# The gate's logits of a decoder layer: sixteen small products in the token loop, or one product for all tokens in the experts' part

## The chip, the cores and the metric

The kernel runs on one core of a Trainium2 chip. The metric is the device time of one execution in microseconds (us). All data and all products are in 32-bit floating point.

## The reference

A decoder layer over 16 sequences of 128 tokens with width 256: self-attention with 16 heads of 64, cross-attention with 16 heads of 16, then a mixture of 8 experts that adds up all experts and scales the sum by a gate. What concerns this change is the gate:

```python
xf = layernorm(x).reshape(-1, D)               # 2048 tokens, D = 256
logits = xf @ gate_w.T + gate_b                # E = 8 per token
ms = jnp.mean(logits * logits, axis=-1, keepdims=True)
logits = logits * jax.lax.rsqrt(ms + eps) * rms_w
gates = jax.nn.softmax(logits / 0.5, axis=-1)
g = gates.max(-1)                              # top 1
norm_g = g / (g + 1e-06)
h = gelu(einsum('nd,edh->neh', xf, w1) + b1)   # H = 512 per expert
y = einsum('neh,ehd->ned', h, w2) + b2
out = (y * norm_g[:, None, None]).sum(axis=1)
```

The logits thus need the normalized tokens and the gate's weights only, and the result `norm_g` is needed where the experts' sum is scaled and written.

## The kernel before, in words

The work is cut by sequence: `b` numbers the 16 blocks of 128 tokens. The kernel has three stretches.

**Slots.** `run_slots(B)` walks 16 slots; slot `s` holds self-attention of block `s`, cross-attention of blocks `s-1` and `s-2`, and the third layer norm of block `s-3`. Each step has a due time within a slot in the table `DUE`, and a heap puts all steps in the order of these times. That order is the program order on PE, DVE, ACT and POOL (`manual_schedule`). `expert_norm` (L670) transposes a normalized block to feature-major form in `xnT` [128, 2, 2048], which all of the experts' products read. `gate_logits(b)` (L678) follows at due time 26.93, after the second half of the keys of the next block (`k1`) and ahead of the cross-attention's keys (`ck`, L505). It makes two products: the 128x128 block of `xnT` stands in PE, and 8 columns of `wgt` move. Its PSUM tile comes from the ring `psum_mm` of four, which all projections and transposes of the slots share. At due time 27.6 DVE adds the bias into `lg[:, b, :]`.

**The written-out tail.** From L889 on the end of the token work (blocks 13 to 15) is laid out by hand between pieces of the experts' first layer (`pre_hidden`, L738) and second layer (`summed_plain`, L880). It holds the last three `gate_logits`. PE and ACT are in program order here, DVE is ordered by the planner.

**Experts.** `experts()` runs four groups `m` of 512 tokens over 16 blocks of hidden features `p`, with Strassen-like products of 256 columns at L993. One round is `hidden_first(p)` (banks `ha`, `hb`, `hf`, `he`; DVE then forms `u` at L1007 to L1009 out of them), part of the previous round's `summed`, `hidden_last(p)` (which adds into `ha`, `hf`, `he`; ACT applies the gelu, DVE forms `c` and the four `t`, L980 to L983), and the rest of `summed`. For `m = 0` the rounds begin at `p = PRE = 8`. Only PE is in program order; ACT, DVE and POOL are ordered by the planner. `gates()` (L692), some twenty small DVE instructions and one on ACT, turns `lg` into `gn` at `p = PRE + 2`; `gn` is first read at L1070 when the first group's sums are written, in group `m = 1`.

`ps_h` has one buffer for each of its banks. `hb` is written by one product a round and read by one DVE instruction (L1007). The weights `wgt` come on SP's DMA queue at L191, ahead of the later token blocks, the output weights `wo` and the experts' weights.

Of the kernel before, what the change touches and what calls it, by code (L numbers as in the profile page):

```python
# [11 lines left out]
F32 = mybir.dt.float32  # L12
# [3 lines left out]
ALU = mybir.AluOpType  # L16
AX = mybir.AxisListType

P = 128
B, T, D = 16, 128, 256  # L20
NT = B * T
KD = D // P
# [6 lines left out]
E, F = 8, 512  # L29
# [5 lines left out]
MT = 512  # L35
# [12 lines left out]
BO1, BO2, GTB, RMS = 0, 256, 512, 520  # L48
# [12 lines left out]
    LN3=18.94, SO=19.16, q1e=19.29, LN3c=19.36, cex0a=19.66, cmax1=19.89, cex0b=21.03,  # L61
    cr0a=21.36, cmul0a=22.23, cex1a=22.4, cr0b=22.6, CO=22.61, xsSO=22.81, bn=23.22,
    cmul0b=23.25, v1=23.47, xsCO=23.72, cex1b=23.78, cr1a=24.06, bn3=24.19, cmul1a=24.34,
    root=24.79, k1=25.19, ve1=25.39, gate=26.93, ke1=27.13, cr1b=27.14, ck=27.19, xn=27.27,
    cmul1b=27.42, lg=27.6, xn3=27.77, cke=28.26, ab2=28.44, early0=6.65, early1=6.7, early=7.9,
    cross=13.9, st0=14.3, st1=14.8, st2=15.6, st3=16.2, st4=17.4, st5=17.9, st6=18.4, st7=18.9,
    st8=20.0, st9=20.5, st10=21.0, st11=21.5, late=31.7,
)
# [5 lines left out]
def decoder_layer(  # L74
# [20 lines left out]
    nc = tc.nc  # L95
# [12 lines left out]
    const = ctx.enter_context(tc.tile_pool(name="const", bufs=1))  # L108
# [19 lines left out]
    def psum_mm(name):  # L128
        return ps_mm.tile([P, 512], F32, tag="mm", name=name)

    ident = const.tile([P, P], F32, tag="ident", name="ident")
# [9 lines left out]
    rowv = const.tile([P, NROW], F32, tag="rowv", name="rowv")  # L141
# [21 lines left out]
    for n, c0 in enumerate((BQ2, BK2)):  # L163
        for m in range(C2):
            for f in range(2):
                nc.gpsimd.dma_start(
                    out=bqk2[64 * f : 64 * f + 64, n, m : m + 1],
                    in_=cols[:, c0 + 2 * m + f : c0 + 2 * m + f + 1].rearrange(
                        "(a s) o -> a s o", s=32
                    )[:, :DH2],  # L170
# [12 lines left out]
    for n, w in ((1, wk2), (0, wq2)):  # L183
        for k in range(KD):
            nc.sync.dma_start(
                out=wx[:, n, k].rearrange("p (h d) -> p h d", d=DH2),
                in_=w[:, k].rearrange("p (h s) -> p h s", s=32)[:, :, :DH2],
            )
    nc.sync.dma_start(out=wx_vo[:, 1], in_=wo2)
    wgt = const.tile([P, KD, E], F32, tag="wgt", name="wgt")  # L190
    nc.sync.dma_start(out=wgt, in_=wg)  # L191

    for b0 in range(4, B, 4):
        load_tokens(b0, 4)
# [22 lines left out]
    xnT = const.tile([P, KD, NT], F32, tag="xnT", name="xnT")  # L217
# [15 lines left out]
    def at(name, f, *a):  # L233


        if now[0] is None:
            f(*a)
        else:
            heapq.heappush(events, (now[0] * SLOT + DUE[name], next(count), now[0], f, a))
# [435 lines left out]
            copy,  # L675
        )

    def gate_logits(b):  # L678
        mm = psum_mm("mm_g")
        for k in range(KD):  # L680
            nc.tensor.matmul(
                mm[:, :E],
                xnT[:, k, b * T : (b + 1) * T],
                wgt[:, k, :],
                start=(k == 0),
                stop=(k == KD - 1),
            )
        at(
            "lg", nc.vector.tensor_tensor, lg[:, b, :], mm[:, :E], rowv[:, GTB : GTB + E], ALU.add
        )  # L690

    def gates():  # L692
# [34 lines left out]
    PRE = 8  # L727
# [20 lines left out]
    def slot(s):  # L748


        for half in range(2):
            at(f"S{half}", self_scores, s, half)
            at(f"SV{'ab'[half]}", self_values, s, half)
            for n in range(2):
                at(f"T1{'ab'[half]}{n + 1}", self_transposed, s, half, n)
                if s >= 2:
                    at(f"T2{'ab'[half]}{n + 1}", cross_transposed, s - 2, half, n)
        at("SO", self_output, s)
        at("cvr", cross_value_rows, s)
        at("ck", cross_keys, s)  # L760
        normalize_outputs(s, s - 2 if s >= 2 else None)
        if s >= 1:
            at("LNx", cross_norm, s - 1)
            at("CQ", cross_queries, s - 1)
            at("CS", cross_scores, s - 1)
            at("CS", cross_softmax, s - 1)
        if s >= 2:
            at("CV", cross_values, s - 2)
            at("CO", cross_output, s - 2)
        if s >= 3:  # L770
            at("LN3", expert_norm, s - 3)
            at("gate", gate_logits, s - 3)
        if s + 2 < B:
            at("xn1", self_norm, s + 2)
            at("ab1", add_bias, s + 2, BO1)
            at("LN1", self_norm_transposed, s + 2)
        if s + 1 < B:
            for n in range(2):
                at(f"q{n}", queries, s + 1, n)
                at(f"k{n}", keys, s + 1, n)  # L780
                at(f"v{n}", values, s + 1, n)
        else:
            for n, name in enumerate(PRE_STEPS):
                copy = nc.vector.tensor_copy if name[0] == "q" else nc.scalar.copy
                out = f"q{name[1]}e" if name[0] == "q" else f"{name[0]}e{name[1]}"
                at(name, pre_hidden, n, copy, out)
        if s == 0:
            mv2 = variances(2)
            for i in range(2):
                at(f"early{i}", statistics, mv2[:, i, :], 2 + i)  # L790
            at("early", lambda: first.update(inverse_deviations(mv2, [2, 3])))
            at("cross", for_cross)
            mv = variances(B - 4)
            for i, name in enumerate(LATE_STATS):
                at(name, statistics, mv[:, i, :], 4 + i)

            def rest():
                first.update(inverse_deviations(mv, list(range(4, B))))

            at("late", rest)  # L800
# [88 lines left out]
    with tc.manual_schedule(  # L889
        engines={mybir.EngineType.PE, mybir.EngineType.Activation}  # L890
    ):
        b = B - 1
        a, v = nc.scalar.copy, nc.vector.tensor_copy
        for h in range(2):
            for n in range(2):
                cross_transposed(b - 1, h, n)
        pre_hidden(6, a)
        cross_values(b - 1)
        pre_hidden(7, a)
        cross_norm(b)  # L900
        cross_output(b - 1)
        expert_norm(b - 2)
        cross_queries(b)
        pre_hidden(8, a)
        cross_scores(b)
        normalize_outputs(None, b - 1)
        gate_logits(b - 2)
        pre_hidden(9, a)
        pre_hidden(10, a)
        cross_softmax(b)  # L910
        pre_hidden(11, v)
        expert_norm(b - 1, v)
        pre_hidden(12, v)
        gate_logits(b - 1)
        pre_hidden(13, v)
        for n in range(2):
            cross_transposed(b, 0, n)
        pre_hidden(14, v)
        pre_hidden(15, v)
        for n in range(2):  # L920
            cross_transposed(b, 1, n)
        scores.close()
        ps_y = ctx.enter_context(
            tc.tile_pool(name="ps_y", bufs=1, space=bass.MemoryType.PSUM, reuse_waits="tile")
        )
        ys = sums()

        def late(p):
            hidden_late(p)
            for k in range(KD):  # L930
                summed_plain(k, p, ys)

        late(0)
        cross_values(b)
        late(1)
        cross_output(b)
        normalize_outputs(None, b)
        late(2)
        late(3)
        expert_norm(b, v)  # L940
        late(4)
        gate_logits(b)
        for p in range(5, PRE):
            hidden_late(p)
    both.close()
# [147 lines left out]
    def experts():  # L1093

        nonlocal ys
        rest = None
        xr = token_factors(0)
        combine(2)  # L1100
        combine(3)
        for p in range(5, PRE - 1):
            for k in range(KD):
                summed_plain(k, p, ys)
        before = None
        for m in range(NT // MT):
            for p in range(0 if m else PRE, NP):
                if m and p == 0:
                    xr = token_factors(m)
                first = hidden_first(p, xr)  # L1110
                if before is None:
                    summed_plain(0, PRE - 1, ys)
                else:
                    if before[0] == 0:
                        ys = sums()
                    summed((1, 2, 3), *before, ys)
                now = p, hidden_last(p, xr, first)
                if before is None:
                    summed_plain(1, PRE - 1, ys)
                else:  # L1120
                    summed((7, 5, 6, 4), *before, ys)
                    if before[0] == NP - 1:
                        rest = finished(m - 1, ys, m == 1)
                if m == 0 and p in (PRE, PRE + 1):
                    combine(p - PRE)
                if m == 0 and p == PRE + 2:
                    gates()
                if p in (1, 2) and rest is not None:
                    rest(p - 1, "he")
                before = now  # L1130
        summed((1, 5, 7, 6, 2, 3, 4), *before, ys)
        rest = finished(m, ys, False)
        for i, bank in enumerate(("hb", "hf")):
            rest(i, bank)
# [67 lines left out]
```

## Time and profile before

| | us |
|---|---|
| runs shown | 879.74, 882.36, 882.36 (median 882.36) |
| profiled execution, its own time | 879.95 |
| profiled execution, span from first to last instruction | 878.2 |
| PE busy / DVE busy / ACT busy / POOL busy | 859.7 / 626.4 / 426.1 / 166.6 |
| gate's products: weight loads, matmuls | 64 each (each product in two passes) |

The profiled execution's time is 1.75 us over its span. PE's granted clock is 0.999. A matmul's duration in the trace holds its latency, and matmuls overlap; what one costs PE in a stream is read from the distance between starts, or from the chain of work that ended last, which is laid out without overlap. In that chain a row has its start, its length, the engine, the tile, the line and the number of instructions. In the timeline a row's length is from the first start to the last end, and a wait stands in brackets. PEld is the weight load, which runs beside the matmul before it. In a row's shape, 128\*32 means that a stationary operand of 128 rows and 32 columns stood in PE.

### The profile page before, as it was taken

Reading aid. Unit: us, or ns where it says so; the run is one execution under the profiler, and the core shown is the slowest. Engines: PE = TensorE matmul, PEld = TensorE weight load, DVE = VectorE, ACT = ScalarE, POOL = GpSimd, SP = SyncE. Lnnn points to the kernel's source line nnn. Section 1 sums busy time; section 2 is a strip of 40 time slices with the busy share of each in tenths; the row PEclk is TensorE's granted clock in tenths of the full one; section 3 lists DMA queues with packets and bytes.
Section 4 is the critical chain, followed back from the end, with each engine's and each line's share of the span. In section 5 each row is a group of like instructions: output and inputs, shape, how many; then the busy total and the mean of one; then the engine's idle time right before and its main releaser. Section 6 shows DMA issues by size and latency. Waiting matters only on the chain.

```text
span 878.2 us, 16053 instructions
## 1 busy us (share of the span) xinstructions
PE 859.7 (98%) x5984; PEld 719.8 (82%) x5984; DVE 626.4 (71%) x1528; ACT 426.1 (49%) x1622; POOL 166.6 (19%) x178
## 2 busy tenths in 40 slices
PE   6999999999999999999999999999999999999997
PEld 5788888888888888888876558878888888878886
DVE  3887787878777787778777489675667656575655
ACT  2366755576556756576553703434333333433332
POOL 4224423343323423342321100000000000000000
PEclk9999999999999999999999999999999999999999
DMA  8800000000000000000051000000000000000000
GB/s 219 253 1 14 1 14 2 2 13 2 8 7 2 13 1 1 14 1 2 6 188 49 13 37 0 1 14 12 1 0 1 25 1 1 0 13 13 1 1 24
DMA packets 19278, 21.30 MB, mean 24 GB/s; under 512 B 9520, under 2 KB 15680, under 8 KB 18560
## 3 DMA queue, kind: packets, MB, share of 16 engines
q1 hardware_dynamic: 17600, 18.89, 6.8%
q10 hardware_dynamic: 1232, 1.09, 0.5%
q8 instruction: 47, 0.77, 0.4%
q0 software_dynamic: 368, 0.30, 0.3%
q14 instruction: 31, 0.25, 0.1%
HBM read 18.16 MB, written 2.10 MB: 23 GB/s over the span
## 4 chain that ended last, share of the span: by engine, by line
PE 92%; DVE 4%; issue 1%; DMA 1%; ACT 1%; POOL 0%; DVEq 0%; ACTq 0%; POOLq 0%
PE y L993 18%; PE mm_qk L389 13%; PE mm_v L428 6%; PE tr_p L366 6%; PE mm_o L488 6%; PE he L993 5%; PE hf L993 5%; PE ha L993 5%; PE sc L444 4%; PE po L468 3%; PE y L880 3%; PE mm_h L738 3%; PE hb L993 3%; PE sc L578 2%; PE po L617 2%; PE mm_k L505 2%
## 5 line engine op out<-in xcount | busy, mean ns | idle before, releaser
L351 POOL TENSOR_TENSOR cpr<-cpr,rinv 128x512 f32<-128x512 f32 x64 | 68.5, 1071 | 221.4 <-DVE rinv L347 221.1
L336 ACT ACTIVATE cpr<-sc,nmax 128x128 f32<-128x128 f32 x256 | 89.9, 412 | 11.6 <-DVE nmax L330 11.6
L336 ACT ACTIVATE pr<-sc,nmax 128x128 f32<-128x128 f32 x256 | 90.8, 420 | 1.8 <-DVE nmax L330 1.8
L330 DVE TENSOR_REDUCE nmax<-sc 128x8 f32<-128x1024 f32 x64 | 76.5, 1215 | 9.7 <-PE sc L444 9.7
L351 POOL TENSOR_TENSOR pr<-pr,rinv 128x512 f32<-128x512 f32 x64 | 66.0, 1043 | 79.1 <-DVE rinv L347 78.7
L1023 DVE TENSOR_TENSOR c<-u,hf 128x256 f32<-128x256 f32 x56 | 23.5, 420 | 72.3 <-PE hf L993 72.3
L1022 ACT ACTIVATE h<-u,colv 128x256 f32<-128x256 f32 x56 | 28.4, 507 | 89.8 <-DVE u L1009 88.1
L389 PEld LDWEIGHTS mm_qk<-xnT,wk 128*128 128x128 f32 x512 | 62.4, 196 | 9.5 <-issue 6.3
L257 ACT COPY xnT<-tr_x 128x256 f32<-128x256 f32 x42 | 15.6, 373 | 111.2 <-PE tr_x L315 111.2
L993 PE MATMUL hf<-xt,w 128*128 128x256 f32 x224 | 66.7, 379 | 0.0
L993 PE MATMUL ha<-xnT,w 128*128 128x256 f32 x224 | 66.6, 379 | 0.0
L993 PE MATMUL y<-t,w 128*128 128x256 f32 x224 | 66.6, 379 | 0.0
L336 ACT ACTIVATION_READ_ACCUMULATOR pr<-sc,nmax 128x1 f32 x256 | 66.3, 259 | 0.0
L389 PE MATMUL mm_qk<-xnT,wk 128*128 128x128 f32 x512 | 64.0, 279 | 1.9 <-DMA wk<-in_wk 1.9
L336 ACT ACTIVATION_READ_ACCUMULATOR cpr<-sc,nmax 128x1 f32 x256 | 64.5, 252 | 0.0
L389 PE MATMUL mm_qk<-xnT,wq 128*128 128x128 f32 x512 | 63.9, 278 | 0.0
L1006 ACT COPY u<-ha 128x256 f32<-128x256 f32 x56 | 20.9, 373 | 87.2 <-PE ha L993 87.2
L389 PEld LDWEIGHTS mm_qk<-xnT,wq 128*128 128x128 f32 x512 | 59.8, 192 | 3.0 <-issue 2.9
L993 PE MATMUL y<-h,w 128*128 128x256 f32 x224 | 58.6, 381 | 1.6 <-DVE yT L1045 1.2
L428 PE MATMUL mm_v<-wv,xnT 128*128 128x512 f32 x128 | 60.2, 592 | 0.0
L488 PE MATMUL mm_o<-wo,atT 128*128 128x256 f32 x256 | 57.9, 379 | 0.0
L257 DVE COPY prT<-tr_p 128x512 f32<-128x512 f32 x64 | 39.7, 682 | 19.3 <-PE tr_p L366 19.3
(164 smaller groups left out, 1880.1 us busy)
## 6 DMA issues: line engine op xcount, KB each, us to landing
w<-in_w SPq DMA_DIRECT2D x8, 1024.0 KB, 5.3
ctx<-in_ctxT SPq DMA_DIRECT2D x8, 256.0 KB, 2.6
out_x<-ot SPq DMA_DIRECT2D x8, 256.0 KB, 2.1
xs<-in_x SPq DMA_DIRECT2D x3, 512.0 KB, 5.8
wk<-in_wk ACTq DMA_DIRECT2D x4, 256.0 KB, 8.7
wq<-in_wq SPq DMA_DIRECT2D x4, 256.0 KB, 10.3
wv<-in_wv SPq DMA_DIRECT2D x2, 512.0 KB, 7.7
wo<-in_wo SPq DMA_DIRECT2D x1, 1024.0 KB, 8.7
```

The source lines that it names most:

```text
L257: f(*a)
L330: nc.vector.tensor_reduce(w["nmax"], sc, AX.X, ALU.max, negate=True)
L336: nc.scalar.activation(w["pr"][:, i, :], sc[:, i, :], AF.Exp, bias=w["nmax"][:, i : i + 1], scale=1.0, accum_out=sums[:, j : j + 1],)
L351: nc.gpsimd.tensor_tensor(four, four, w["rinv", n].unsqueeze(2).broadcast_to([P, 4, T]), ALU.mult)
L366: nc.tensor.transpose(tr[:, j, :], w["pr"][:, 4 * n + j, :], ident)
L389: nc.tensor.matmul(mm[:, i, :], w[:, k, c * P : (c + 1) * P], xnT1[:, k, 0, :], start=(k == 0), stop=(k == KD - 1),)
L428: nc.tensor.matmul(mm, entry["xnT1", b][:, k, 0, :], wv[:, k, f], start=(k == 0), stop=(k == KD - 1),)
L444: nc.tensor.matmul(sc[:, j, c * T : (c + 1) * T], qT[r, 4 * half + c, :], kT[r, 4 * half + c, :], start=True, stop=True,)
L468: nc.tensor.matmul(po[j * DH1 : (j + 1) * DH1, c, :], v[:, h * DH1 : (h + 1) * DH1], prT[:, 4 * j + c, :], start=True, stop=True,)
L488: nc.tensor.matmul(mm[:, :D], atT[:, c, :], wo[:, c, :], start=(c == 0), stop=(c == C1 - 1))
L993: nc.tensor.matmul(out, left[p // q][n - 1][:, p % q], rights[n - 1], **flags)
L1022: nc.scalar.activation(h[:, 1, 1], u[:, 3], AF.Gelu, bias=col(B1 + 2 * p + 1))
```

## The change

The sixteen `gate_logits(b)` are gone, with their sixteen bias additions on DVE and their entries in `DUE`. `wgt` is widened to 32 columns for each half of the features, zeroed by POOL, and its first 8 columns are loaded. In the experts' part, for `m = 0`, after `hidden_last(PRE + 2)`, one `gate_logits()` makes all logits: the 128x32 weights stand in each of four column quarters of PE, and quarter `r` gets the 512 tokens of group `r` as its moving operand, so that the four quarters fill the four partition quarters of one PSUM bank (`hb`). ACT copies the bank to SBUF. One round later, after `hidden_last(PRE + 3)`, four transposes bring the logits back to token-major form in `hb`, and one DVE instruction adds the bias into all of `lg`. `gates()` moves from `p = PRE + 2` to `p = PRE + 3`.

```diff
-    wgt = const.tile([P, KD, E], F32, tag="wgt", name="wgt")
-    nc.sync.dma_start(out=wgt, in_=wg)
+    wgt = const.tile([P, KD, 32], F32, tag="wgt", name="wgt")
+    nc.gpsimd.memset(wgt, 0.0)
+    nc.sync.dma_start(out=wgt[:, :, :E], in_=wg)
...
-    def gate_logits(b):
-        mm = psum_mm("mm_g")
+    def gate_logits():
+        mm = ps_h.tile([P, MT], F32, tag="hb", name="mm_g")
         for k in range(KD):
-            nc.tensor.matmul(
-                mm[:, :E],
-                xnT[:, k, b * T : (b + 1) * T],
-                wgt[:, k, :],
-                start=(k == 0),
-                stop=(k == KD - 1),
-            )
-        at(
-            "lg", nc.vector.tensor_tensor, lg[:, b, :], mm[:, :E], rowv[:, GTB : GTB + E], ALU.add
+            for r in range(4):
+                nc.tensor.matmul(
+                    mm[32 * r : 32 * r + 32, :],
+                    wgt[:, k, :],
+                    xnT[:, k, r * MT : (r + 1) * MT],
+                    start=(k == 0),
+                    stop=(k == KD - 1),
+                    tile_position=(0, 32 * r),
+                )
+        lgT = yp.tile([P, MT], F32, tag="yT", name="lgT")
+        nc.scalar.copy(lgT, mm)
+        return lgT
+
+    def gate_transposed(lgT):
+        tr = ps_h.tile([P, 4, P], F32, tag="hb", name="tr_g")
+        for i in range(4):
+            nc.tensor.transpose(tr[:, i, :], lgT[:, i * T : (i + 1) * T], ident)
+        nc.vector.tensor_tensor(
+            lg.rearrange("p (r i) e -> p i r e", i=4),
+            tr.rearrange("p i (r w) -> p i r w", w=32)[:, :, :, :E],
+            rowv[:, GTB : GTB + E].unsqueeze(1).unsqueeze(1).broadcast_to([P, 4, 4, E]),
+            ALU.add,
         )
...
         if s >= 3:
             at("LN3", expert_norm, s - 3)
-            at("gate", gate_logits, s - 3)
...
         normalize_outputs(None, b - 1)
-        gate_logits(b - 2)
         pre_hidden(9, a)
...
         pre_hidden(12, v)
-        gate_logits(b - 1)
         pre_hidden(13, v)
...
         late(4)
-        gate_logits(b)
...
                 now = p, hidden_last(p, xr, first)
+                if m == 0 and p == PRE + 2:
+                    lgT = gate_logits()
+                if m == 0 and p == PRE + 3:
+                    gate_transposed(lgT)
...
-                if m == 0 and p == PRE + 2:
+                if m == 0 and p == PRE + 3:
                     gates()
```

More of the change, by code (lines that the diff above doesn't have):

```diff
@@ L63 @@
     cmul0b=23.25, v1=23.47, xsCO=23.72, cex1b=23.78, cr1a=24.06, bn3=24.19, cmul1a=24.34,
-    root=24.79, k1=25.19, ve1=25.39, gate=26.93, ke1=27.13, cr1b=27.14, ck=27.19, xn=27.27,
-    cmul1b=27.42, lg=27.6, xn3=27.77, cke=28.26, ab2=28.44, early0=6.65, early1=6.7, early=7.9,
+    root=24.79, k1=25.19, ve1=25.39, ke1=27.13, cr1b=27.14, ck=27.19, xn=27.27,
+    cmul1b=27.42, xn3=27.77, cke=28.26, ab2=28.44, early0=6.65, early1=6.7, early=7.9,
     cross=13.9, st0=14.3, st1=14.8, st2=15.6, st3=16.2, st4=17.4, st5=17.9, st6=18.4, st7=18.9,
```

## The prediction

> **What bounds the kernel now.** I read the page first (the engines' shares, the chain that ended last), then the chain in single stretches, then the groups by shape, then the timelines of PE and DVE where the new work goes.
>
> ```profile
> span 878.2 us, 16053 instructions
> ...
> PE 859.7 (98%) x5984; PEld 719.8 (82%) x5984; DVE 626.4 (71%) x1528; ACT 426.1 (49%) x1622; POOL 166.6 (19%) x178
> ...
> PE 92%; DVE 4%; issue 1%; DMA 1%; ACT 1%; POOL 0%; DVEq 0%; ACTq 0%; POOLq 0%
> ```
>
> PE is the chain nearly everywhere. What PE no longer does is time saved, except where the 4% of DVE lie. A steady slot, in the chain:
>
> ```profile
> 267.16 0.35 PE mm_g L681 x4
> 267.50 0.99 PE mm_k L505 x8
> ...
> 277.03 0.89 PE mm_q L556 x8
> ...
> 279.65 1.75 PE tr_p L366 x16
> ```
>
> The gate has 0.35 us, and the eight products behind it have 0.99, where the same eight-product shape (mm_q) without a gate ahead has 0.89. In slot 2, which has no gate yet, mm_k itself has
>
> ```profile
> 96.84 0.89 PE mm_k L505 x8
> ```
>
> So one gate costs 0.35 + 0.10 = 0.45 us of PE. A check on whole slots: self-attention's scores start at 69.87, 97.67 and 126.13, so the slot without gate and without the third norm's transposes took 27.80 and the next one 28.46; the difference, 0.66, is the gate's 0.45 and two transposes of 0.11.
>
> Two places are DVE's. In the last slot the chain runs on DVE from 450.5 to 468.4:
>
> ```profile
> 450.52 1.34 DVE prT L257 x3
> ...
> 466.80 0.97 DVE xn L306
> 467.78 0.61 DVE cprT L245
> 468.52 0.63 PE tr_p L366 x4
> ```
>
> And in the experts' first rounds DVE works without a gap from 509.8 to 549.2 (weight combinations, then gates()), and once PE waits for it:
>
> ```profile
> 531.29 0.70 PE L993 MATMUL he<-xnT,w1c 128*128 128x256 f32 x2 [0.23 <-DVE u L1009]
> ```
>
> **What is removed.** Slots 3 to 14: 12 x 0.45 = 5.40. Nothing takes the gate's place there: DVE waits for the scores at the slot's head (0.44 us idle ahead of nmax at 269.6), and its own work ahead of that shrinks too, since the bias addition (158 ns, 0.08 from its start to the next one's) goes; the keys' copy on ACT (267.19 to 268.33) would still be done ahead of the second half of the scores (from 269.4, then 269.0). Taking a tile out of the PSUM ring of four only makes later tiles wait for earlier releases.
>
> Slot 15's gate lies at 465.5 within the DVE chain: only the 0.08 of DVE counts. The three gates of the tail: 0.34 each plus the slower start of what follows, as in
>
> ```profile
> 497.30 1.01 PE po L617 x32
> 498.31 3.63 PE y L880 x8
> ...
> 513.32 0.34 PE mm_g L681 x4
> 513.67 6.97 PE y L880 x16
> ```
>
> where 16 passes at 0.43 would be 6.88: 0.43 together. Likewise 0.43 at 478.8 and 0.44 at 486.5. (The first shows 0.54, but 0.20 of it is the way from the row-tiled scores, which the next product will pay.) Sum 1.30. Between the last scores and their transposes PE loses 0.87 of cover; POOL's half-0 product ends at 487.93 and its transposes start at 488.94, so 1.0 of margin remains 0.1 to 0.3. Removed in all: 5.40 + 0.08 + 1.30 = 6.8 us.
>
> Given back: the last gate lies after DVE's unbroken stretch has begun, which itself shrinks by 0.07 only. At 531.29 PE already waits, so 0.43 - 0.07 = 0.36 turns into a longer wait there.
>
> **Here a rule speaks against the change.** The row first: four gate passes of 8 columns take 0.45 us, 0.11 each, while their 128-column weight loads are
>
> ```profile
> L681 PEld LDWEIGHTS mm_g<-wgt,xnT 128*128 128x128 f32 x64 | 8.7, 192 | 1.8 <-issue 1.0 <-ACT pre L245 0.3 <-DVE root_t L278 0.2
> L681 PE MATMUL mm_g<-wgt,xnT 128*128 128x8 f32 x64 | 8.3, 237 | 0.0
> ```
>
> The Trainium skill's page "TensorEngine Tiling (Array Packing)", section Performance Considerations, Instruction Overhead, says that a matmul has about 60 cycles of overhead, so that one of 1 column takes as long as one of 60; at the 2.4 GHz that "TensorE: Matmul & The Clock Gate" states that is 25 ns. By it the 64 passes would be worth 1.6 us, and the change would lose about 1.6 us (1.6 removed, 3.2 added and given back). The row decides: the distance is 0.11, the weight load's, and I take 0.45.
>
> **What is added on PE.** Eight products in two passes, 16 passes of 512 columns at 0.43 (3.44 for eight y passes): 6.9 us one after the other. The nearest row for four column quarters is the cross-attention's values, 128\*32, also with the quarter as the inner loop: 32 passes in 1.01 us, starts 0.026 apart, where a 128-column pass alone needs 0.108. So four run at a time. Sixteen passes / 4 x 0.43 = 1.72, and the way into and out of the quarters: 1.01 - 32 x 0.108 / 4 = 0.15 before, 3.63 - 3.44 = 0.19 after. Together 2.06. The skill gives less on column tiles: "TensorE: Matmul & The Clock Gate", Part 3, Measured speedup, has 2.38 for three and 3.07 for four row tiles. With 3.07 it would be 2.25 + 0.34 = 2.6. I take the row, 2.06; 512 moving columns in four quarters are shown nowhere, so the ends are 1.9 and 7.2.
>
> Four transposes: 4 x 1.75 / 16 = 0.44.
>
> **Waits added.** (a) Round 11's product into hb waits until ACT has copied the logits (0.59 for 128x512). Between them PE has four y products and ha, 1.73 + 0.43 = 2.16; on ACT the copy stands behind round 10's gelus, which end 0.5 to 1 us ahead of it. Nothing; were ACT held 1.3 us longer, it would show. (b) Round 12's product into hb waits for the DVE addition out of hb (about 0.3, from the 128x128 gate rows at 284 to 292 ns). Behind hidden_last PE has 0.44 + 2.16. A later round shows where PE and DVE would be (timeline of each):
>
> ```profile
> 549.53 0.59 PE L993 MATMUL he<-xnT,w1c 128*128 128x256 f32 x2
> ...
> 552.12 0.59 PE L993 MATMUL hb<-xt,w1c 128*128 128x256 f32 x2
> ```
>
> ```profile
> 551.16 0.42 DVE L980 TENSOR_TENSOR t<-h 128x256 f32<-128x256 f32 x1 [0.57 <-ACT h L1026]
> ...
> 552.29 0.42 DVE L983 TENSOR_TENSOR t<-h,t 128x256 f32<-128x256 f32 x1
> ```
>
> Placed in the 0.57 of idle time ahead of the t's it costs nothing; behind the last t it ends near 553.0, where hb would be due at 552.56: 0.5 to 0.8 with the signal. I take 0.3. Queued behind it on DVE are the t's (next round's sums) and u. gates(), about 7 us of dependent small steps, moves from round 10 to 11 or 12, with DVE less loaded than now, and is needed some 25 us later: nothing. The new products read weights and tokens that have long been there.
>
> **At the start.** POOL's clearing of wgt comes at 10.8, ahead of the 128x1088 clears (1.02 each): about 0.1, covered, as POOL then waits 4.45 for DVE. SP's load at 23.66 now waits for that clear, 12 us after it: nothing. It has twice the pieces, 0.43 to perhaps 0.9 us of issue. Behind it stand token blocks, wo (issued 25.7, 8.7 to land, used at 37.65: 3.2 of margin), a context and the experts' weights. Nothing; if wo were late, the excess over 3.2.
>
> **Sum.** -6.8 + 0.36 + 2.06 + 0.44 + 0.3 = -3.6 us. The profiled execution took 879.95 (span 878.2 and 1.75 around it): 876.3. The median shown lies 2.4 above the profiled time, the mean of the three shown 1.5; I add 1.6 and say 878.
>
> **Rivals.**
> 1. *Half of the gain is eaten* (slots or DVE take it up: slot 15's chain spreads, the wide quarters reach 3 instead of 4, hb's wait is 0.8): -6.8 + 0.9 + 2.6 + 0.44 + 0.8 = -2.1, or 879.5; with less of the slots, 880.5. For: the margins at the tail's transposes and ahead of nmax are tenths. Against: the with-and-without slots.
> 2. *The quarters run one after the other*, slower than before: 6.9 + 0.34 in place of 2.06 at round 10. -3.6 + 5.2 = +1.6: 883. It decides when fewer than 1.5 passes run at a time. Against it stands L617; for it, that four wide moving streams of 128 partitions are untried.
> 3. *gates() goes as a block ahead of u (L1007)* in DVE's queue, as the planner orders it: 7.2 less the 1.3 of slack and 0.6 of idle, PE waits 5.3: +1.7, 883. It decides from 3.6 us of wait. Against: before, the planner threaded u between the gate's steps.
> 4. The change doing nothing it says can be excluded: the sixteen calls go.
>
> **Chances.** About 0.3% (2.6 us) is what a measurement here can tell from no change. The forecast 0.58, nearly all beyond 0.3%; rival 1 0.24, within it; rivals 2 and 3 0.07 and 0.06, and an unseen cost 0.05: half of these beyond 0.3% when measured, with the likeliest unseen cost in DVE's order. That gives faster 0.58, same 0.30, slower 0.12. The forecast's own range is 875 to 880; with rivals 1 and part of 2 and 3 the range is 874.5 to 882.5.
>
> **What would show it.** Right: no mm_g in the slots, mm_k at 0.89, score starts 28.0 apart; in round 10 a block of 16 passes 128\*32 with starts 0.11 apart and some 2.1 us in the chain; four tr_g at 0.11; a wait of at most 0.8 at hb in round 12; a longer wait at he in round 9. Wrong: starts 0.43 apart in the block, slots still 28.4 apart, or PE waiting microseconds for u or hb.

## The result, and the profile after

| | before | after |
|---|---|---|
| median of six runs, us | 882.0 | 877.83 |
| ratio, with its 95% interval | | 0.9959 (0.9946 to 0.9972) |
| profiled execution: time, span | 879.95, 878.2 | 877.13, 875.3 |

The change makes the kernel 0.41% faster (0.28 to 0.54), 3.6 us by the ratio; the medians alone are 4.2 apart. The two profiled executions differ by 2.8 (time) and 2.9 (span).

The lines of the page after the change that answer to the first fence of the prediction:

```profile
span 875.3 us, 15944 instructions
...
PE 856.2 (98%) x5940; PEld 713.6 (82%) x5940; DVE 627.5 (72%) x1513; ACT 425.5 (49%) x1623; POOL 166.8 (19%) x179
...
PE 89%; DVE 7%; issue 1%; ACT 1%; DMA 1%; POOL 0%; DVEq 0%; ACTq 0%; POOLq 0%
```

PE has lost 3.5 us of busy time and is as full as before; the chain leans on DVE for 7% in place of 4%, and most of the added share lies in the experts' first rounds. A steady slot in the chain of the kernel after (start, length, engine, tile, line):

```profile
265.10 0.89 PE mm_k L506 x8
265.99 1.99 PE sc L445 x32
...
294.00 1.99 PE sc L445 x32
```

The gate is gone, the keys behind it take 0.89, and the scores (`sc`) of two slots start 28.01 apart. The chain through DVE in the last slot has gained nothing:

```profile
461.21 1.40 DVE xn L307 x2
462.61 0.61 DVE cprT L246
463.35 0.63 PE tr_p L367 x4
```

The last two of these rows stand 5.17 us earlier than the same two in the prediction (467.78 and 468.52). That is what the twelve slots ahead had saved, 5.33, less the 0.16 by which this execution began later, and no more: DVE's 0.08 us did not show. The new block with the row ahead of it in round 9, again in the chain:

```profile
525.86 1.73 PE y L1004 x8
...
531.91 1.85 PE mm_g L684 x16
533.76 1.92 PE y L1004 x8
```

Sixteen passes take 1.85, and the eight passes of `y` behind them 1.92, where the same eight take 1.73 in round 9. In round 8, PE's timeline before and after:

```profile
524.35 0.59 PE L993 MATMUL hf<-xt,w 128*128 128x256 f32 x2
524.78 0.61 PE L993 MATMUL he<-xnT,w1c 128*128 128x256 f32 x2
```

```profile
517.84 0.59 PE L1004 MATMUL hf<-xt,w 128*128 128x256 f32 x2
518.55 0.70 PE L1004 MATMUL he<-xnT,w1c 128*128 128x256 f32 x2
```

The product into `he` came 0.43 after the one into `hf`, as in an unbroken stream; now it comes 0.71 after it. Later, with the waits in brackets:

```profile
525.16 0.70 PE L1004 MATMUL he<-xnT,w1c 128*128 128x256 f32 x2 [0.23 <-DVE u L1020]
...
539.84 0.60 PE L699 MATMUL tr_g<-ident,lgT 128*128 128x128 f32 x4
...
542.44 0.59 PE L1004 MATMUL hb<-xt,w1c 128*128 128x256 f32 x2
...
548.05 0.59 PE L1004 MATMUL ha<-xnT,w 128*128 128x256 f32 x2
...
552.10 0.70 PE L1004 MATMUL hf<-xt,w 128*128 128x256 f32 x2 [0.43 <-DVE u L1019]
...
554.88 0.59 PE L1004 MATMUL ha<-xnT,w 128*128 128x256 f32 x2
```

The wait in round 9, at 525.16, is the 0.23 that stood there before. The transposes cost their 0.44, the product into `hb` in round 12 follows without a wait, and in round 13 (548.05 to 554.88) PE waits for DVE where it did not before.

A table of where the time went, by starts in PE's timeline. A round runs from one product into `ha` that is followed by `hb` to the next such product. An undisturbed one takes 6.04; round 8, which has eight passes of 512 columns, takes 6.46 without any wait.

| stretch | before | after | difference | predicted |
|---|---|---|---|---|
| start of slot 3's scores | 97.67 | 97.83 | +0.16 | 0 |
| twelve slots to slot 15's scores | 341.30 | 335.97 | -5.33 | -5.40 |
| from there to round 8 | 81.50 | 80.17 | -1.33 | -1.38 |
| round 8 | 6.47 | 6.84 | +0.37 | +0.36 (in round 9) |
| rounds 10 and 11: block, transposes | 12.08 | 14.57 | +2.49 | +2.50 |
| round 12: wait at hb | 6.05 | 6.05 | 0.00 | +0.30 |
| round 13 | 6.04 | 6.83 | +0.79 | 0 |
| sum to round 14 | | | -2.85 | -3.62 |

### The profile page after: what moved, and what is told of

Read it like the earlier page. It is cut to its first block, busy times and chain, and to the rows that moved or that the text cites. A ratio compares the mean times of both kernels' runs of the same rounds, so it can differ in the third digit from the quotient of the medians.

```text
span 875.3 us, 15944 instructions
## 1 busy us (share of the span) xinstructions
PE 856.2 (98%) x5940; PEld 713.6 (82%) x5940; DVE 627.5 (72%) x1513; ACT 425.5 (49%) x1623; POOL 166.8 (19%) x179
## 4 chain that ended last, share of the span: by engine, by line
PE 89%; DVE 7%; issue 1%; ACT 1%; DMA 1%; POOL 0%; DVEq 0%; ACTq 0%; POOLq 0%
PE y L1004 18%; PE mm_qk L390 13%; PE mm_v L429 6%; PE tr_p L367 6%; PE mm_o L489 6%; PE he L1004 5%; PE hf L1004 5%; PE ha L1004 5%; PE sc L445 4%; PE po L469 3%; PE mm_h L753 3%; PE hb L1004 2%; PE sc L579 2%; PE po L618 2%; PE mm_q L557 2%; PE y L894 2%
```

## Experiments

The first 50 us differ by up to 4 us from one execution to the next whatever the kernel, which the section on the hardware explains. So the rounds and slots of the traces carry the verdicts here, and the ratios to the kernel before stand beside them where a kernel was run several times.

**The gates removed, nothing added.** Only the removal half of the change; `lg` is a constant, so the logits are left out.

```diff
+    nc.gpsimd.memset(lg, 0.5)
...
-            at("gate", gate_logits, s - 3)
...
-        gate_logits(b - 2)
...
-        gate_logits(b - 1)
...
-        gate_logits(b)
```

> The kernel before without its sixteen gate products and bias additions; the logits are a constant 0.5 set once, the rest including gates() in round 10 stays. Theory (PE is the bound, a gate is worth its four weight loads): 12 slots x 0.445, three in the tail x 0.44, nothing for the gate of slot 15, less 0.36 waited back at he in round 8 or 9: -6.3 us against before, slot 3 to 4 starts 28.0 apart instead of 28.46. Rival (a gate is worth its 8 moving columns[...]): -1.6 us. Rival (slots absorb it): slots stay over 28.2.

Ratio 0.9927 (0.9914 to 0.9940), or -6.4 us. In its chain:

```profile
268.05 1.99 PE sc L445 x32
...
296.06 1.99 PE sc L445 x32
```

In the trace the slots 3 to 13 are 28.01 or 28.02 long (28.46 before) and slot 14 is 27.79 (28.24), slot 15's scores to round 8 take 80.17 and round 8 takes 6.84: -5.3, -1.3 and +0.4, as in the table. A gate is worth 0.44, four times the 0.11 of a pass and not the 0.1 of the first rival; slots absorb nothing, except slot 15. One thing differs from what was expected: since the logits are a constant, the planner put gates() at 10.9 us and not in round 10. So the rounds 10 to 13 of this kernel, all at 6.04, say nothing about gates().

**The block and the transposes added, nothing removed.** The old gates stay in force, and the new logits go to a scratch tile; `gate_all` is the change's `gate_logits` with weights `wgp` of its own.

```diff
+    wgp = const.tile([P, KD, 32], F32, tag="wgp", name="wgp")
+    nc.gpsimd.memset(wgp, 0.0)
+    nc.sync.dma_start(out=wgp[:, :, :E], in_=wg)
...
+                if m == 0 and p == PRE + 2:
+                    lgT = gate_all()
+                if m == 0 and p == PRE + 3:
+                    gate_transposed(lgT)
```

> The kernel before with all its gates, plus the new block of 16 passes in round 10 and the four transposes and bias addition in round 11, which write a scratch tile that nothing reads; gates() stays in round 10. Theory (four quarters at a time): +2.05 for the block and +0.43 for the transposes, and no wait at round 13, since gates() is not moved: +2.5 us. Rival (gates() in its new place, not the block, is what costs DVE time at round 13): then this kernel shows no wait at hf in round 13. If the wait is there too, it comes from the addition's place on DVE.

In its chain:

```profile
540.07 1.85 PE mm_g L701 x16
541.92 1.92 PE y L1025 x8
...
548.16 0.44 PE tr_g L716 x4
```

Ratio 1.0024 (1.0016 to 1.0031), +2.1 us. Round 10 takes 8.09, round 11 6.48, round 13 6.04: +2.05, +0.44, and no wait. The two halves, -6.4 and +2.1, leave -4.3; the whole change measured -3.6. Within the intervals that is no contradiction. The 0.79 of round 13 appears in neither half: it comes only when gates() has to follow the new block.

**Does the order of the quarters matter?** The two loops of the block exchanged.

```diff
-        for k in range(KD):
-            for r in range(4):
+        for r in range(4):
+            for k in range(KD):
```

> The changed kernel with the block's loops exchanged: quarter outside, half of the features inside, so that the four passes of one quarter follow one another. Theory A (each quarter has its own queue, all sixteen passes are in sight at once): the block stays at about 1.85 us in the chain and 2.05 with the way out. Theory B (passes start strictly in order, and the next quarter starts only when the last pass of the one before has started): three passes of each quarter are waited for, 4 x 3 x 0.43 + 0.43 = 5.6 us, and the kernel is 3.7 us slower than the changed one.

In its chain:

```profile
531.33 1.87 PE mm_g L684 x16
```

1.87 against 1.85, and round 10 at 8.12 against 8.10. The number is theory A's: four passes of one quarter in a row hold up the other quarters no more than four quarters in turn. How PE queues the passes, the rows do not show.

**All products in one quarter.** The price of the rival in which the quarters do not run side by side. Three of four groups of logits are left out, and the two loops are exchanged as above.

```diff
-                    mm[32 * r : 32 * r + 32, :],
+                    mm[0:32, :],
...
-                    tile_position=(0, 32 * r),
+                    tile_position=(0, 0),
...
-        nc.scalar.copy(lgT, mm)
+        nc.gpsimd.memset(lgT, 0.0)
+        nc.scalar.copy(lgT[0:32], mm[0:32, :])
```

> The changed kernel with all eight products in the first column quarter, one group of tokens after the other over the same 32 partitions of the bank; only the last group's logits remain in it, the other rows are zero. Theory (passes of one quarter run one after the other): 16 x 0.43 = 6.9 us, 5.1 us more than the block in four quarters, the product into hb still covered, so span 875.3 + 5.1 = 880.4, slower than before by 2.2. Rival (the moving columns overlap also within a quarter): the block stays near 2 us.

In its chain:

```profile
531.42 6.99 PE mm_g L684 x16
538.41 1.92 PE y L1005 x8
```

6.99 for what four quarters do in 1.85, a factor of 3.8. Round 10 is 13.22, 5.13 longer than in the changed kernel, and the span is 880.0 (880.4 expected) against 878.2 in the trace of the kernel before.

**Sixteen times the moving columns.** The kernel before, with its gate weights padded to 128 moving columns.

```diff
-    wgt = const.tile([P, KD, E], F32, tag="wgt", name="wgt")
-    nc.sync.dma_start(out=wgt, in_=wg)
+    wgt = const.tile([P, KD, 128], F32, tag="wgt", name="wgt")
+    nc.gpsimd.memset(wgt, 0.0)
+    nc.sync.dma_start(out=wgt[:, :, :E], in_=wg)
...
-                mm[:, :E],
+                mm[:, :128],
```

> The kernel before with its gate weights widened to 128 moving columns by zeros, sixteen times as many moving columns in each of the 64 passes; the additions read the first 8 as before. Theory (a gate pass costs its 128-column weight load, 0.11, and up to 128 moving columns are covered by it): chain rows of the gate and the keys after it still sum to about 1.34, span within 0.7 us of 878.2. Rival (the moving columns count on top: 120 more at 0.84 ns each, 0.10 a pass): 64 x 0.10 = 6.4 us more, 884.6.

In its chain:

```profile
265.95 0.45 PE mm_g L682 x4
266.39 0.89 PE mm_k L506 x8
```

0.45 + 0.89 = 1.34, as 0.35 + 0.99 with 8 columns, and slots of 28.46 in both. The span, 877.0, is 0.5 under the expected range, since slot 0's scores start 1.2 earlier there. A pass with a 128-column stationary operand takes 0.11 whether 8 or 128 columns move. That is why the change pays: what stood in PE, 128 columns of tokens, now moves, in four quarters at once. That the 0.11 is the weight load, and not another floor under every pass, is the prediction's reading; no run here has a narrow stationary operand with few moving columns, which would part the two.

**Without gates().** The gate's steps from the logits to the scale are left out.

```diff
-                    gates()
+                    nc.vector.tensor_copy(gn, lg[:, :, 0])
```

> The changed kernel without the steps of gates(): the scale of the output is a plain copy of the first expert's logit, made after the addition. Theory (the wait at hf and he in round 13 comes from gates() on DVE): both waits are 0, span 0.75 us below the changed kernel's 875.3, 874.6; the waits at he in rounds 8 and 9 stay. Rival (round 13 waits for another reason, such as the block's shift of PE against DVE): the waits of 0.4 to 0.6 stay.

Round 13, between its first and the next round's first product in PE's timeline:

```profile
549.44 0.59 PE L1004 MATMUL ha<-xnT,w 128*128 128x256 f32 x2
...
555.49 0.59 PE L1004 MATMUL ha<-xnT,w 128*128 128x256 f32 x2
```

Round 13 takes 6.05, round 8 still 6.84, rounds 10 and 11 8.10 and 6.48. The wait comes from gates(). The span, 876.0, missed the expected 874.6, since slot 0 took 25.92 there and 24.30 in the changed kernel.

**The block ahead of round 8.** Where DVE is behind.

```diff
+        lgT = gate_logits()
         before = None
...
-                if m == 0 and p == PRE + 2:
-                    lgT = gate_logits()
```

> The changed kernel with the block of 16 passes moved from round 10 to just before round 8, where DVE is behind with the weight combinations; transposes and gates() stay in round 11. Theory (PE waits for DVE in rounds 8 and 9, 0.27 + 0.10 + 0.23 in all): the block gives DVE 2.05 us to catch up, so these waits go: about -0.6 us against the changed kernel, -4.2 against before, unless the wait grows at round 13. Rival (the waits follow PE because DVE's order is tied to PE's): no gain, the same -3.6.

Ratio 0.9957 (0.9945 to 0.9970), no different from the changed kernel's. Round 9 takes 6.09 (6.62), so that wait has gone; round 8 takes 6.96, since a new one has come:

```profile
515.84 0.59 ACT lgT L693
516.43 0.04 issue
516.47 0.70 PE hb L1004 x2
```

The product into `hb` now has only the 0.43 of `ha` between itself and the block, and waits for ACT's copy. From slot 15's scores to the end of round 10 it is 101.21 against 101.73: 0.5 gained. Round 13 stays at 6.84.

**Part of gates() on POOL.** Seven of its elementwise steps.

```diff
-        nc.vector.tensor_tensor(lg, lg, each(ms), ALU.mult)
+        nc.gpsimd.tensor_tensor(lg, lg, each(ms), ALU.mult)
...
```

> The changed kernel with seven of the elementwise steps of gates() on POOL, which is idle from 492 us on (square, both scalings, difference from the maximum, 1 + t, 1 - t, product); reductions, the inverse root and the reciprocals stay on DVE. Theory (round 13 waits because gates() holds DVE): some 1.9 us of DVE work leaves, and the waits of 0.60 and 0.15 at hf and he in round 13 shrink to 0 to 0.3: -0.5 us against the changed kernel. Rival (the chain of dependent steps, with DVE queued in order behind POOL's steps, gets longer and blocks u): waits of 1 us and more in rounds 12 to 14, slower than the changed kernel.

Ratio 0.9957 (0.9942 to 0.9973), which does not tell it from the changed kernel. In the trace round 13 takes 7.56, 0.73 longer than there: the rival. In its chain:

```profile
547.56 0.96 DVE sq L729
...
548.63 0.50 POOLq L1213
...
551.52 0.70 PE hf L1004 x2
```

The chain goes through POOL and back to DVE, where the reciprocal waits 0.84 for POOL with t and u behind it in the queue.

**gates() two rounds later in the program.**

```diff
-                if m == 0 and p == PRE + 3:
+                if m == 0 and p == PRE + 5:
                     gates()
```

> The changed kernel with gates() two rounds later, in round 13 in place of 11; block and transposes stay. Theory (gates() is a chain of about 7 us of small DVE steps that holds up the same round's additions wherever DVE has only about 2.3 us of free time a round): the wait moves along, some 0.8 us in round 15, none in round 13. Rival (round 13's wait comes from the backlog that round 11's addition left): no wait anywhere, 0.8 us less.

Neither theory, though the number is near the rival's. Round 13 takes 6.20, round 15 6.04: no wait moved along. The planner starts gates() at 541.3 in this kernel, where the logits are ready, and not two rounds later; only the order within DVE's queue is another one, as its timeline shows:

```profile
549.79 0.42 DVE L994 TENSOR_TENSOR t<-h,t 128x256 f32<-128x256 f32 x1
550.13 0.94 DVE L729 RECIPROCAL sq<-sq 128x128 f32<-128x128 f32 x1
```

The longest step of gates(), the reciprocal, stands behind round 12's four t's here. In the changed kernel it stands ahead of them:

```profile
548.23 0.95 DVE L729 RECIPROCAL sq<-sq 128x128 f32<-128x128 f32 x1
...
549.18 0.41 DVE L991 TENSOR_TENSOR t<-h 128x256 f32<-128x256 f32 x1
...
551.62 0.42 DVE L1019 TENSOR_TENSOR u<-u,hf 128x256 f32<-128x256 f32 x1
```

**That one step made short.** The new theory: what PE waits for in round 13 is this reciprocal. DVE's order stays the same.

```diff
-        nc.vector.reciprocal(sq, sq)
+        nc.vector.reciprocal(sq[:, 0], sq[:, 0])
```

> The changed kernel with the reciprocal of 1 + t in gates() taken over one block's 8 values in place of all 128; the other blocks' gates are computed from 1 + t itself. DVE's order stays as it is. Theory (the 0.95 us of this reciprocal, which stands ahead of round 12's four t's in DVE's queue, hold up t, then u, then PE at hf in round 13): about 0.75 less on DVE there, round 13 from 6.83 to 6.04 to 6.15. Rival (gates() as a whole, some 7 us of steps, is too much for DVE's free time in two rounds): round 13 stays above 6.5.

Round 13 in PE's timeline:

```profile
550.46 0.59 PE L1004 MATMUL ha<-xnT,w 128*128 128x256 f32 x2
...
556.57 0.59 PE L1004 MATMUL ha<-xnT,w 128*128 128x256 f32 x2
```

The step takes 0.20, and round 13 6.11 in place of 6.83: 0.72 of the 0.79 goes with this step's length, as the theory had it.

Its place in the queue is not the whole cause. In the kernel before, the reciprocal stands ahead of four t's too, and PE does not wait (DVE's timeline, then PE's):

```profile
544.85 0.94 DVE L714 RECIPROCAL sq<-sq 128x128 f32<-128x128 f32 x1
...
545.79 0.41 DVE L980 TENSOR_TENSOR t<-h 128x256 f32<-128x256 f32 x1
```

```profile
545.64 0.59 PE L993 MATMUL ha<-xnT,w 128*128 128x256 f32 x2
```

There it starts 0.79 ahead of the round that it could hold up; in the changed kernel 0.18 behind that round's start (548.23 against 548.05), and with POOL 0.81 behind it (547.56 against 546.75). The round grows by 0, 0.79 and 1.52. gates() begins later against its first round: 2.1 us into it before (535.70), when the logits have long been ready, and 5.3 us into it after (540.80), behind the addition that makes them. Its steps up to the reciprocal then follow closer (7.4 us in place of 9.2), which makes good only a part.

**One round earlier.**

```diff
-                if m == 0 and p == PRE + 2:
+                if m == 0 and p == PRE + 1:
                     lgT = gate_logits()
-                if m == 0 and p == PRE + 3:
+                if m == 0 and p == PRE + 2:
                     gate_transposed(lgT)
```

(and gates() in round 10)

> The changed kernel with the block in round 9, the transposes, addition and gates() in round 10. Theory (the wait depends on how the planner threads gates() between the additions, and behind the weight combinations it threads them later and thinner, as in the kernel before): round 8 stays at 6.84, round 9 grows by the block's 2.05, round 10 by 0.44, and no wait of over 0.2 in rounds 11 to 13: 0.8 us less than the changed kernel. Rival (7 us of steps cost 0.8 wherever the logits come fresh from PE): 0.6 to 0.8 in round 12.

The rival: rounds 8 to 12 take 6.84, 8.67, 6.48, 6.04 and 6.83. The wait comes two rounds behind the transposes again, and the reciprocal again starts 0.17 behind the round's start.

**All of it early.** The block ahead of the last four second-layer products before round 8, transposes in round 9, gates() in round 10.

```diff
         for p in range(5, PRE - 1):
+            if p == PRE - 2:
+                lgT = gate_logits()
...
-                if m == 0 and p == PRE + 2:
-                    lgT = gate_logits()
-                if m == 0 and p == PRE + 3:
+                if m == 0 and p == PRE + 1:
                     gate_transposed(lgT)
...
-                if m == 0 and p == PRE + 3:
+                if m == 0 and p == PRE + 2:
                     gates()
```

> The changed kernel with the block ahead of the last four second-layer products before round 8 (so that ACT's copy lies under 3.4 us of PE and hb is free in round 8), the transposes and the addition in round 9 and gates() in round 10, the round it had in the kernel before. Theory (PE waits 0.37 + 0.58 for DVE in rounds 8 and 9 and 0.79 in round 13; the block's 2.05 us cover the first, gates() in round 10 avoids the last): rounds 8 to 13 sum to 6 x 6.04 + 0.44 + at most 0.4 = 37.1 against 40.9 less 2.05 for the block = 38.9, so 1.7 us under the changed kernel, 0.6% under the one before. Rival (DVE is behind in round 9, so that the addition out of hb comes late): PE waits 1 us or more at hb in round 10, and nothing is gained.

Rounds 8 to 13 take 6.45, 6.93, 6.04, 6.05, 6.04 and 6.04, together 37.55; the changed kernel's 40.91 less the block's 2.05 are 38.86. So it is 1.3 us less, with one wait for DVE left in round 9, where the round is 0.45 over its 6.04 and the transposes' 0.44:

```profile
526.24 0.70 PE L1004 MATMUL he<-xnT,w1c 128*128 128x256 f32 x2 [0.18 <-DVE u L1020]
526.77 0.60 PE L699 MATMUL tr_g<-ident,lgT 128*128 128x128 f32 x4
```

The expectation of 1.7 had a slip: it allowed 0.4 for such a wait, but took round 8 at 6.04, where its own passes take 6.46. The span is 873.6, the lowest of all kernels that compute the gate in full. Its ratio to the kernel before, 0.9959 (0.9941 to 0.9976), is that of the changed kernel: 1.3 us is less than these intervals can tell, so by time it is not shown to be the better one.

## Why the prediction was right, point by point

- *The gates removed: -6.8, less 0.36.* The trace has -6.66 and +0.37. The 0.45 for a gate was 0.44, and DVE's 0.08 did not come. The place of the 0.36 was a round off: the wait grew in round 8, not in round 9.
- *The rule that spoke against the change*, of the Trainium skill's "TensorEngine Tiling (Array Packing)", Performance Considerations, Instruction Overhead, gave an estimate of 1.6 us for the gates by 60 cycles for a small matmul. Removing them brought 6.4, so the row decided rightly; the padded gate shows that with 128 stationary columns the moving ones do not count up to 128. Whether the load is what sets the 0.11, as the prediction says, is not shown.
- *The block: 2.06.* Measured 2.05, with the switch into and out of the quarters. Four wide moving streams run side by side as four narrow ones do, to a factor of 3.8. The starts come in fours within 0.02 us, the fours 0.43 apart, not evenly 0.11 apart as the prediction had it; the sum is the same. The 3.07 for four row tiles in the Trainium skill's "TensorE: Matmul & The Clock Gate", Part 3, Measured speedup, would have given an estimate of 2.6, which is too much here.
- *The transposes: 0.44.* Measured 0.43 to 0.44.
- *The wait (b) at hb, 0.3.* It was zero: the planner put the addition at 540.5, directly behind round 11's c and ahead of its t's, which is the cheap one of the two places weighed. The 0.3 lay between the two.
- *gates() moved: nothing.* This step failed, by 0.79. The reasoning was that DVE is less loaded in round 11 than in round 10 and that the result is needed late. Both are so; but gates(), 27 steps on DVE, could now begin only behind the new addition, and so its 0.95 us step, ahead of the t's in DVE's order, came 0.97 later against PE's rounds than before and held up t, then u, then PE. Rival 3 had this mechanism and priced it at 5.3 for the whole of gates(); it came with a seventh of that. Among the chances, an unseen cost, likeliest in DVE's order, had 0.05.
- *The start: nothing.* POOL's clear takes 0.17 at 10.55, SP's load of the weights 0.55 in place of 0.43 and is issued at 23.8; nothing waits for either.
- Together: the sum of -3.62 against -2.85 in the trace, where the gap of 0.77 is round 13's 0.79, less the 0.30 that did not come, with 0.16 at the start and 0.12 that the gates brought less; and -3.6 in the ratio. That the ratio meets the sum is partly luck: its interval is 2.3 us wide, and, as the section on the hardware shows, like executions of the two kernels differ by 2.8 or by 3.6. The 878 was met by luck too: the profiled execution took 877.13 and not 876.3, and the median lay 0.7 above it and not 1.6; the two misses cancel.
- The rivals: serial quarters were measured (one quarter, +5.1) and are not what happens. Of the 1.5 us that the first rival took off the forecast, 0.8 are missing in the trace, but at none of the places it named: the slots at 28.01 do not absorb the gain, the quarters run at 3.8 and `hb` does not wait.

## What to carry to other kernels

In this kernel a product with 8 moving columns cost PE as much as one with 128. Such a product can be turned round, so that the few columns stand and the many move, and four of them put side by side in column quarters: 64 passes of 0.11 became 16 that take 0.13 each with the switches, and four transposes. Price what such a change moves on the other engines' queues as well. Here not the 7 us of moved work set the wait but its longest single step, what stood behind it in the queue, and how late it came for PE's round. Look for a place where the bounding engine waits for another anyway; added work there is partly free, as the 1.3 us of the last experiment show.

## What the runs showed of the hardware that was not expected

The first slots vary whatever the kernel does: over the 14 traces slot 0 takes either 24.3 us (8 traces) or 25.9 (6), and slot 0's scores start anywhere from 20.05 to 22.38. The cause of the first is PE's granted clock; that of the second stays open. PE waits about 1.5 us for POOL, until 32 to 34 us, in all of them; in six the clock is lower behind it. The columns are the stretch, its length, busy time of PE, PEld, DVE, ACT and POOL with the instructions counted, and then the granted clock; first the kernel with the gates removed, then the kernel before:

```profile
34.00:36.00 2.00, 2.00 (x16) 1.67 (x16) 1.92 (x9) 0.37 (x1) 0.41 (x1) 0.53 1.02 403
```

```profile
34.00:36.00 2.00, 2.00 (x34) 1.83 (x33) 1.88 (x11) 0.37 (x1) 0.00 (x0) 1.00 1.04 406
```

A clock of 0.53 against 1.00, and half as many passes. In all six traces the stretch is one of 3.41 us at 0.50, as here, again with the gates removed:

```profile
34.14:37.50 3.36, 3.36 (x29) 3.03 (x29) 3.21 (x14) 0.37 (x1) 0.27 (x1) 0.50 1.03 411
37.60:38.60 1.00, 1.00 (x14) 0.83 (x11) 0.97 (x4) 0.00 (x0) 0.00 (x0) 1.00 1.07 426
```

Half of 3.41 is 1.7, and slot 0 is 1.6 longer. The Trainium skill's page "TensorE: Matmul & The Clock Gate", Part 1, tells of a gate that halves the clock after an idle window of about 3.4 us, where the windows run freely. The length of the stretch, and that it falls on some executions only, fit; the wait of 1.5 us ahead of it is shorter than the page's window, and no run here varied it.

The stretch costs more than half of what the whole change brought in the trace. The mean clock of an execution tells whether it had it: 0.996 or 0.997 in the six traces with it, 0.998 or 0.999 in the others. The changed kernel's six executions are three of each kind, 876.9 to 877.5 us and 878.2 to 878.9. Of 27 executions of the kernel before, run beside the experiments, eight are at 0.998 or 0.999, with a mean of 880.0, and nineteen below, with 882.1. So like against like the change brings 2.8 us without the stretch, which is the difference of the two profiled executions, and 3.6 with it. Why the kernel before loses more by it, no trace shows. Stretches behind the start are therefore better compared than single times and spans.
